# Attention output divided without transposes: denominators sent through DMA, SyncE queue in source order

## Chip, cores, metric

The kernel runs on one core of a Trainium2 chip. The metric is the device time of one execution in microseconds, median of three runs. TensorE is written PE below, VectorE DVE, ScalarE ACT, GpSimd POOL, SyncE SP.

## What is computed

Eight sequences of 512 tokens with 512 channels go through a "macaron" block: half a feed-forward layer, attention, half a feed-forward layer, each behind a layer norm and added to its input.

```python
x = x + 0.5 * ffn(layernorm(x))        # ternary weights, silu(gate) * up, rms norm
x = x + attention(layernorm(x))        # 32 heads of 16 channels, window of 128 keys back
x = x + 0.5 * ffn(layernorm(x))
# attention, for each head and block of 128 queries:
probs = softmax(where(valid, q @ k.T / 4, min))
out   = (probs @ v) @ Wo.T
```

The softmax is computed as weights exp(score - maximum). Their products with v, and their sum (the denominator), come out of the same matmul; the output is the product divided by the denominator. The change is about where that division is done.

## The kernel before

There are three stages. Stage a (first feed-forward) writes `rows_a` to HBM, stage b (attention) reads `rows_a` and writes `rows_b`, and stage c (second feed-forward) reads `rows_b`. All matmuls are fp32 or fp32 in split terms.

Stage b treats the 8 sequences (index `b`) by groups of 8 heads (index `j`, 4 to a sequence): 32 groups `i`. A group has four units `u`, one for each block of 128 queries (index `t`), so there are 128 units. The source is one loop over `u`, a software pipeline written out by hand. One pass of the loop, called a step here, emits in this order:

- `probabilities(u)`: PE forms score tiles `sp` (line 798). ACT takes three and DVE one of the four out of PSUM (lines 810 and 806), ACT takes the exponential (812), POOL zeroes what lies outside the window in two halves (817).
- `weighted(u - 1)`: PE multiplies the weights by `vones`, which holds 16 columns of v and 16 columns of ones for each head, into `av` (833). In this way 16 rows of `av` are the product and 16 rows the denominator, 32 rows for each of 4 heads. Each second unit ACT copies `av` to `ab` (842).
- `maxima(u + 6)`: PE forms the scores `sm` (750), and DVE takes their maximum in 8 instructions named `seen` (758), each followed by a short read of the accumulator.
- one long product of 8 matmul instructions (line 677), by `t`: values (`wv`) at t = 0, output (`wo`) at t = 1, queries (`wq`) at t = 2, keys (`wk`) at t = 3. The queries and keys are for group `i + 3`; they are split in two terms by ACT and DVE (690, 691), and SP issues four DMAs `qs` (708) or four DMAs `ks` (720) that interleave them over partitions.
- after each second unit `turned` (851): four PE transposes of `ab` into `abT`; `divided` (857, 861): DVE takes reciprocals of the denominators and multiplies four times; and one step later `turned_back` (873, 876): two PE transposes back, and an ACT copy into `oT`.
- `row_loaded(b + 2)` (641): an SP DMA that loads 1 MB of `rows_a` into `x_b`, at j = 0, t = 3. `x_b` has one buffer. The layer norm of it begins in the next step (j = 1, t = 0) with `st_b` on DVE (204), and goes on over j = 1 and 2.
- `output(b - 1, j)` at t = 1: `wo` reads `oT`, DVE adds the residual `xr` (890), SP stores to `rows_b` (891).

Score tiles, transposes and the `neg` transposes (777) share six PSUM buffers `ps_s`, given out in turn; `av` and the long products have one each.

PE, DVE, ACT and POOL run the loop in source order (`manual_schedule`). SP is not in that list: the framework's scheduler places SP's DMAs. On every engine instructions run strictly in the built order, so a waiting instruction holds up all behind it. DMAs take one of eight completion semaphores in turn, so each DMA also waits for the one eight before it.

Of the kernel before, what the change touches and what calls it, by code (L numbers as in the profile page):

```python
# [8 lines left out]
F32 = mybir.dt.float32  # L9
# [3 lines left out]
ALU = mybir.AluOpType  # L13
AX = mybir.AxisListType

P = 128
# [8 lines left out]
def macaron_block(  # L25
# [19 lines left out]
    nc = tc.nc  # L45
# [41 lines left out]
    rows_b = [dram.tile([P, TB, D], F32, name=f"rows_b{b}") for b in range(B)]  # L87
    wgu_kept = [dram.tile([P, 2 * DC, P], F32, name=f"wgu_kept{c}") for c in range(FC)]
    h_kept = [dram.tile([P, T], F32, name=f"h_kept{c}") for c in range(FC)]
    wp_kept = [dram.tile([P, 2, D], F32, name=f"wp_kept{u}") for u in range(FC // 2)]  # L90

    PSUM = bass.MemoryType.PSUM

    def pool(stack, name, bufs, space=bass.MemoryType.SB):

        return stack.enter_context(
            tc.tile_pool(name=name, bufs=bufs, space=space, reuse_waits="tile")
        )
# [511 lines left out]
    def attention_stage():  # L610
# [16 lines left out]
        }  # L627
        ring = pool(s, "ring_b", 3)
        probs = pool(s, "probs_b", 3)
        opool = pool(s, "o_b", 7)  # L630
        work = pool(s, "work_b", 3)

        ps_s = pool(s, "ps_s", 6, PSUM)
# [11 lines left out]
        attn_w = {}  # L645
        for name, src in (("wv", wv_t), ("wq", wq_t), ("wk", wk_t), ("wo", wo_t)):
            attn_w[name] = fixed[name].tile([P, DC, D], F32, name=f"{name}_sb")
            nc.sync.dma_start(attn_w[name], src.rearrange("(c p) e -> p c e", p=P))
        vones = [
            fixed[f"vones{i}"].tile([P, TB, N_HEADS, 2 * DK], F32, name=f"vones{i}_sb")  # L650
            for i in range(2)
# [6 lines left out]
        for h in range(2):  # L658
            nc.vector.tensor_copy(selects[h], max_rows[h].to_broadcast([P, P]))
        for tile_ in vones:  # L660
            nc.gpsimd.memset(tile_[:, :, :, DK:], 1.0)
        for tile_ in terms_of_negs:
            nc.gpsimd.memset(tile_.bitcast(F32), 0.0)

        xrs = {}
        abTs, qs, ks, ms, pTs, avs, abs_, os_, oTs = {}, {}, {}, {}, {}, {}, {}, {}, {}
        NJ = DC
        units = B * NJ * TB

# [3 lines left out]
        def sum_of_products(name, pairs, done):  # L673
            space, tag = (ps_mm, "mm") if 0 <= u < units else (ps_s, "s")
            ps = space.tile([P, T], F32, tag=tag, name=name)
            for n, (lhs, rhs) in enumerate(pairs):
                nc.tensor.matmul(ps, lhs, rhs, start=(n == 0), stop=(n == len(pairs) - 1))  # L677
            done(ps)
# [45 lines left out]
        def values(b, t):  # L724
            rows = slice(t * P, (t + 1) * P)
            pairs = [(xss[b][:, k, rows], attn_w["wv"][:, k, :]) for k in range(DC)]
            sum_of_products(
                f"wv_{b}_{t}", pairs,
                lambda ps: nc.vector.tensor_copy(
                    vones[b % 2][:, t, :, :DK], ps.rearrange("p (h d) -> p h d", d=DK)  # L730
                ),
            )

        def scores_tile(name):
            return [
# [87 lines left out]
        def weighted(u):  # L823

            i, t = u // TB, u % TB
            b, j = i // NJ, i % NJ
            if t % 2 == 0:
                avs[i] = ps_av.tile([P, 2, 2, P], F32, tag="av", name=f"av_{u}")
            for h in range(2):
                blocks = [(t - 1, 1), (t, 0)] if t else [(t, 0)]  # L830
                for n, (block, m) in enumerate(blocks):
                    for g in range(NG):
                        nc.tensor.matmul(  # L833
                            avs[i][32 * g : 32 * g + 32, h, t % 2, :],
                            vones[b % 2][:, block, NG * (2 * j + h) + g, :],
                            pTs[u - t + block][:, 2 * g + h, m * P : (m + 1) * P],
                            start=(n == 0), stop=(n == len(blocks) - 1),
                        )

            if t % 2 == 1:  # L840
                abs_[i] = work.tile([P, 2, 2, P], F32, tag="ab", name=f"ab_{u}", bufs=2)
                nc.scalar.copy(abs_[i], avs.pop(i))

        def turned(u):

            i, t = u // TB, u % TB
            pt = abTs[i] = ps_s.tile([P, 2, 2, P], F32, tag="s", name=f"abT_{u}")
            ab = abs_.pop(i)
            for m in range(2):
                for h in range(2):  # L850
                    nc.tensor.transpose(pt[:, m, h, :], ab[:, h, m, :], ident)  # L851

        def divided(u):
            i, t = u // TB, u % TB
            rows = abTs.pop(i).rearrange("p m h (g r) -> p (m h) g r", r=32)
            rden = small.tile([P, 4, NG, 1], F32, tag="rden", name=f"rden_{u}")
            nc.vector.reciprocal(rden, rows[:, :, :, DK : DK + 1])
            os_[i] = work.tile([P, 2, 2, NG, DK], F32, tag="o", name=f"o_{u}", bufs=2)
            for m in range(2):
                for h in range(2):  # L860
                    nc.vector.tensor_tensor(
                        os_[i][:, m, h], rows[:, 2 * m + h, :, :DK],
                        rden[:, 2 * m + h].to_broadcast([P, NG, DK]), ALU.mult,
                    )

        def turned_back(u):
            i, t = u // TB, u % TB
            if t == 1:
                oTs[i] = opool.tile([P, T], F32, tag="oT", name=f"oT_{i}")
            o = os_.pop(i)  # L870
            back = ps_s.tile([P, 2, P], F32, tag="s", name=f"oTp_{u}")
            for m in range(2):
                nc.tensor.transpose(
                    back[:, m, :], o[:, m].rearrange("p h g d -> p (h g d)"), ident
                )
            nc.scalar.copy(
                oTs[i][:, (t - 1) * P : (t + 1) * P], back.rearrange("p m q -> p (m q)")
            )

        def residual_loaded(b, t):  # L880
            xrs[b, t] = work.tile([P, D], F32, tag="xr", name=f"xr_{b}_{t}")
            nc.scalar.dma_start(xrs[b, t], rows_a[b][:, t, :])

        def output(b, t):
            xr = xrs.pop((b, t))
            rows = slice(t * P, (t + 1) * P)
            pairs = [(oTs[NJ * b + j][:, rows], attn_w["wo"][:, j, :]) for j in range(NJ)]

            def done(ps):
                nc.vector.tensor_tensor(xr, ps, xr, ALU.add)  # L890
                nc.sync.dma_start(rows_b[b][:, t, :], xr)

            sum_of_products(f"wo_{b}_{t}", pairs, done)
# [2 lines left out]
        row = NJ * TB  # L896
        engines = {
            mybir.EngineType.PE, mybir.EngineType.DVE, mybir.EngineType.Activation,
            mybir.EngineType.Pool,
        }  # L900
        s.enter_context(tc.manual_schedule(engines=engines))
        for u in range(-row - row // 2 - 2, units + row):
            i, t = u // TB, u % TB
            b, j = i // NJ, i % NJ
            if b == -2 and j == 2:
                with tc.high_priority():
                    if t == 0:
                        for block in range(TB):
                            norms[0][0](block)
                    for part in norms[0][1:]:  # L910
                        part(t)
            if 0 <= u < units:
                probabilities(u)
            if 0 <= u - 1 < units:
                weighted(u - 1)
            if t == 0 and 0 <= b - 1 < B:
                residual_loaded(b - 1, j)
            ended = u - 1 + AHEAD
            if 0 <= ended < units and ended % TB == TB - 1:

                maxima_split(ended // TB)
            if 0 <= u + AHEAD < units:
                maxima(u + AHEAD)
            if j in (1, 2) and 0 < b + 2 < B:
                norms[b + 2][j - 1](t)

            if 0 <= ended < units and ended % TB == TB - 1:
                maxima_turned(ended // TB)
            if b == -1 and j >= 2 and t < 2:
                values(0, 2 * (j - 2) + t)  # L930
            if t == 0 and 0 < b + 1 < B:
                values(b + 1, j)
            if t == 1 and 0 <= b - 1 < B:
                output(b - 1, j)
            if t == 2 and 0 <= i + 3 < B * NJ:
                queries(i + 3)
            if t == 3 and 0 <= i + 3 < B * NJ:
                keys(i + 3)
            turned_b, turned_t = divmod(u - 1, row)
            turned_t -= 2 * TB  # L940
            if 0 <= turned_t < TB and 0 < turned_b + 2 < B:
                norms[turned_b + 2][2](turned_t)
            if 0 <= u - 1 < units and (u - 1) % 2 == 1:
                turned(u - 1)
                divided(u - 1)
            if 0 <= u - 2 < units and (u - 2) % 2 == 1:
                turned_back(u - 2)
            if j == 0 and t == 3 and 0 < b + 2 < B:
                row_loaded(b + 2)
        s.close()  # L950
# [32 lines left out]
```

## Time and profile before

| | us |
|---|---|
| median of 3 runs (2469.08 to 2471.29) | 2469.84 |
| the profiled execution | 2469.46 |
| its span, first to last instruction | 2467.4 |
| mean granted PE clock | 0.98 of full |
| busy: PE, DVE, ACT, POOL | 2379.9, 1339.4, 982.2, 861.8 |

The span runs from the first to the last instruction; the execution is 2.06 us longer. Stage b lies between about 800 us, when stage a's last rows are ready, and 1719 us, when stage c's first rows are loaded. In the profile lines, `x8` is a count of instructions, and a name such as `abT<-ident,ab` is output from inputs.

### The profile page before, as it was taken

To read this page: it belongs to the slowest core of one execution; us is meant where nothing else is said; L and a number is where in the kernel's file an instruction comes from. 1 tells how busy PE (TensorE), PEld (TensorE's weight loads), DVE (VectorE), ACT (ScalarE), POOL (GpSimd) and SP (SyncE) were. 2 spreads that over 40 slices of the span, in tenths; PEclk is the share of its full clock that TensorE was granted. 3 is DMA by queue.
4 is the path that set the end of the run, shared out by engine and by line. 5 is a ranking of instruction groups with operands and counts; after the bars stand their busy time and mean duration, and the time that the engine had idled before them with its cause. 6 is when DMAs were issued, how large, how long until landed. Compare 5 with 4: busy or idle time off the path is not lost.

```text
span 2467.4 us, 43216 instructions
## 1 busy us (share of the span) xinstructions
PE 2379.9 (96%) x17208; PEld 1777.0 (72%) x17208; DVE 1339.4 (54%) x3929; ACT 982.2 (40%) x1476; POOL 861.8 (35%) x714
## 2 busy tenths in 40 slices
PE   5999999999999999999999999987899999999998
PEld 4778888888887466666666666654788888888887
DVE  7884443443444676766767676662444453453442
ACT  6773222222221355665556566554222222222221
POOL 0000344444445132323223232222344444444544
PEclk8999999999999999999999999988899999999999
DMA  4433010000011523323332332353100000100000
GB/s 162 157 135 135 35 35 1 35 35 1 35 52 37 143 58 84 105 74 95 83 95 74 96 91 74 78 159 135 58 35 1 35 35 1 35 35 1 35 18 17
DMA packets 63192, 160.58 MB, mean 65 GB/s; under 512 B 7440, under 2 KB 11536, under 8 KB 59920
## 3 DMA queue, kind: packets, MB, share of 16 engines
q1 hardware_dynamic: 47680, 116.68, 16.4%
q10 hardware_dynamic: 15312, 41.16, 4.5%
q8 instruction: 135, 2.21, 0.4%
q14 instruction: 65, 0.53, 0.1%
HBM read 66.32 MB, written 41.16 MB: 44 GB/s over the span
## 4 chain that ended last, share of the span: by engine, by line
PE 92%; DVE 3%; ACT 2%; issue 1%; DMA 0%; POOL 0%; ACTq 0%; POOLq 0%; DVEq 0%; SPq 0%
PE gu_c L281 19%; PE gu_a L281 17%; PE o_a L316 9%; PE o_c L316 9%; PE sp L798 5%; PE wk L677 5%; PE wv L677 5%; PE av L833 5%; PE wo L677 5%; PE wq L677 5%; PE sm L750 4%; PE abT L851 1%; PE neg L777 1%; ACT pT L812 1%; PE ptn_c L225 1%
## 5 line engine op out<-in xcount | busy, mean ns | idle before, releaser
L281 PE MATMUL gu_a<-xs_a,wgu_a 128*128 128x512 f32 x2048 | 493.3, 394 | 7.2 <-ACT sg_a L292 3.0
L281 PE MATMUL gu_c<-xs_c,wgu_c 128*128 128x512 f32 x2048 | 490.1, 392 | 0.7 <-ACT xs_c L228 0.7
L817 POOL TENSOR_SCALAR_AFFINE_SELECT pT<-pT 128x1024 f32<-128x1024 f32 x224 | 242.8, 1104 | 628.6 <-ACT pT L812 628.6
L281 PEld LDWEIGHTS gu_a<-xs_a,wgu_a 128*128 128x128 f32 x2048 | 383.6, 189 | 90.1 <-ACT sg_a L292 4.3
L281 PEld LDWEIGHTS gu_c<-xs_c,wgu_c 128*128 128x128 f32 x2048 | 383.1, 188 | 80.1 <-ACT xs_c L228 1.1
L758 DVE CUSTOM_DVE_ANT_0 seen<-sm,window 128x256 f32<-128x256 f32 (+1 forms) x1024 | 331.3, 388 | 87.4 <-PE sm L750 86.6
L316 PE MATMUL o_a<-wp_a,hs_a 128*128 128x512 f32 x1024 | 256.6, 396 | 0.0
L316 PE MATMUL o_c<-wp_c,hs_c 128*128 128x512 f32 x1024 | 251.6, 389 | 0.0
L297 DVE TENSOR_TENSOR h_c<-gu_c,sg_c 128x512 f32<-128x512 f32 x128 | 88.3, 690 | 277.9 <-PE gu_c L281 275.7
L587 POOL TENSOR_TENSOR sq_c<-h_c 128x512 f32<-128x512 f32 x120 | 124.9, 1041 | 316.5 <-DVE h_c L297 303.1
L810 ACT ACTIVATE pT<-sp 128x512 f32<-128x512 f32 (+1 forms) x384 | 181.2, 545 | 129.6 <-PE sp L798 129.6
L316 PEld LDWEIGHTS o_a<-wp_a,hs_a 128*128 128x128 f32 x1024 | 193.3, 190 | 40.0 <-DVE hs_a L306 0.2
L812 ACT ACTIVATE pT<-pT 128x2048 f32<-128x2048 f32 (+1 forms) x128 | 217.3, 1698 | 10.9 <-DVE pT L806 7.6
L316 PEld LDWEIGHTS o_c<-wp_c,hs_c 128*128 128x128 f32 x1024 | 192.2, 188 | 39.9
L297 DVE TENSOR_TENSOR h_a<-gu_a,sg_a 128x512 f32<-128x512 f32 x128 | 88.3, 689 | 230.2 <-PE gu_a L281 225.6
L588 POOL TENSOR_TENSOR ss_c<-ss_c,sq_c 128x512 f32<-128x512 f32 x120 | 192.1, 1601 | 8.9
L292 ACT ACTIVATE sg_c<-gu_c 128x512 f32<-128x512 f32 x128 | 76.6, 599 | 263.9 <-PE gu_c L281 248.6
L302 ACT CAST hs_c<-h_c 128x512 fp32r<-128x512 f32 x128 | 79.5, 621 | 250.2 <-DVE h_c L297 250.1
L587 POOL TENSOR_TENSOR sq_a<-h_a 128x512 f32<-128x512 f32 x90 | 94.1, 1045 | 229.9 <-DVE h_a L297 220.7
L306 DVE TENSOR_TENSOR hs_c<-h_c,hs_c 128x512 fp32r<-128x512 f32 x128 | 124.1, 969 | 83.1 <-ACT hs_c L302 83.1
L292 ACT ACTIVATE sg_a<-gu_a 128x512 f32<-128x512 f32 x128 | 76.4, 597 | 212.3 <-PE gu_a L281 202.8
L302 ACT CAST hs_a<-h_a 128x512 fp32r<-128x512 f32 x115 | 71.3, 620 | 202.4 <-DVE h_a L297 200.0
(137 smaller groups left out, 3128.1 us busy)
## 6 DMA issues: line engine op xcount, KB each, us to landing
ks<-k SPq DMA_DIRECT2D x128, 256.0 KB, 4.9
qs<-q SPq DMA_DIRECT2D x128, 128.0 KB, 2.4
wf_gu<-w_gate_up_dram SPq DMA_DIRECT2D x16, 512.0 KB, 3.5
wgu_kept<-wgu_a ACTq DMA_DIRECT2D x16, 512.0 KB, 2.7
rows_a<-x_a ACTq DMA_DIRECT2D x8, 1024.0 KB, 3.9
x_b<-rows_a SPq DMA_DIRECT2D x8, 1024.0 KB, 5.4
xr<-rows_a ACTq DMA_DIRECT2D x32, 256.0 KB, 5.4
rows_b<-xr SPq DMA_DIRECT2D x32, 256.0 KB, 2.1
```

Source lines behind the costliest of these rows:

```text
L281: nc.tensor.matmul(ps, wgu[c][:, i * DC + k, :], xss[b][:, part, k, :], start=(k == 0 and part == 0), stop=(k == DC - 1 and part == 1),)
L292: nc.scalar.activation(sg, gate, AF.Silu)
L297: nc.vector.tensor_tensor(h, up, sg, ALU.mult)
L302: nc.scalar.copy(hs[:, 0, :], h)
L316: nc.tensor.matmul(ops[t], hs[:, part, t * P : (t + 1) * P], wp[e // 2][:, e % 2, :], start=(e == begin and part == 0), stop=(e == end and ...
L587: nc.gpsimd.tensor_tensor(sq, h, h, ALU.mult)
L588: nc.gpsimd.tensor_tensor(sumsq, sumsq, sq, ALU.add)
L677: nc.tensor.matmul(ps, lhs, rhs, start=(n == 0), stop=(n == len(pairs) - 1))
L758: nc.vector.tensor_tensor_reduce(out=seen[:, : n * P], in0=tiles[g][:, h, : n * P], in1=window[:, (2 - n) * P :], scale=-1.0, scalar=3.4e3 ...
L810: nc.scalar.activation(under, tiles[g][:, :, : n * P], AF.Relu, scale=-1.0)
L812: nc.scalar.activation(seen, seen, AF.Exp, scale=-1.0)
L817: nc.gpsimd.affine_select(out=half, in_=half, compare_op=ALU.is_ge, fill=0.0, base=0, pattern=[[0, 2 * NG], [sign, P]], channel_multiplier ...
```

## The change

- `vones` holds v and ones in alternate columns: v first for half of the heads (h = 0), ones first for the others. Its memset covers the whole tile, and the copy of `wv` into it becomes two strided copies of half the size. Product rows of h = 0 then lie on even partitions of `av`, those of h = 1 on odd ones.
- `turned`, `divided` on DVE, and `turned_back` are gone. ACT copies `av` into `sums`, one tile for a whole group.
- Once for each group, SP sends one denominator row per head to HBM (`dens`, two DMAs) and both halves of the product rows into one tile `oT` (two DMAs of 128 KB); loads the denominators back as 128 x 32 (`den`); DVE takes 128 x 32 reciprocals; SP writes them to HBM (`inverses`) and reads each row back 16 times over into `rep` (eight DMAs of 32 KB); POOL multiplies `oT` by `rep`. These stand one or two steps apart, over the two groups that follow.
- Output products come two groups later, and the loop is eight steps longer. `wo` is loaded in two halves with rows in the new order. `oT` has 9 buffers (7 before), `xr` 2 (3 before).
- SP joins the engines whose order is that of the source.

```diff
-        opool = pool(s, "o_b", 7)
+        opool = pool(s, "o_b", 9)
...
-            nc.gpsimd.memset(tile_[:, :, :, DK:], 1.0)
+            nc.gpsimd.memset(tile_, 1.0)
...
+            def kept(ps):
+                heads = vones[b % 2][:, t].rearrange("p (j h g) d -> p h j g d", h=2, g=NG)
+                made = ps.rearrange("p (j h g d) -> p h j g d", h=2, g=NG, d=DK)
+                for h in range(2):
+                    nc.vector.tensor_copy(heads[:, h, :, :, h::2], made[:, h])
...
             if t % 2 == 1:
-                abs_[i] = work.tile([P, 2, 2, P], F32, tag="ab", name=f"ab_{u}", bufs=2)
-                nc.scalar.copy(abs_[i], avs.pop(i))
...
+                if t == 1:
+                    sums[i] = work.tile([P, 2, T], F32, tag="sums", name=f"sums_{i}", bufs=2)
+                nc.scalar.copy(
+                    sums[i][:, :, (t - 1) * P : (t + 1) * P],
+                    avs.pop(i).rearrange("p h m q -> p h (m q)"),
                 )
+        def rows_of(t, h):
+            return t.rearrange("(r two) t -> r two t", two=2)[:, h]
+        def denominators(i):
+            taken = sums.pop(i)
+            for h in range(2):
+                nc.sync.dma_start(
+                    dens[i % 2][h],
+                    taken[:, h].rearrange("(g r) t -> g r t", r=32)[:, 1 - h],
+                )
+            oTs[i] = opool.tile([P, T], F32, tag="oT", name=f"oT_{i}")
+            for h in range(2):
+                nc.sync.dma_start(rows_of(oTs[i], h), rows_of(taken[:, h], h))
+        def denominators_back(i):
+            den = dens_sb[i] = work.tile([P, T // DK], F32, tag="den", name=f"den_{i}", bufs=1)
+            nc.sync.dma_start(den, dens[i % 2].rearrange("h g (s e) -> (h g s) e", s=DK))
+        def inverted(i):
+            inv = work.tile([P, T // DK], F32, tag="inv", name=f"inv_{i}", bufs=1)
+            nc.vector.reciprocal(inv, dens_sb.pop(i))
+            nc.sync.dma_start(inverses[i % 2].rearrange("h g (s e) -> (h g s) e", s=DK), inv)
+        def spread(i, h):
+            if h == 0:
+                reps[i] = work.tile([P, T], F32, tag="rep", name=f"rep_{i}", bufs=1)
+            rows = rows_of(reps[i], h)
+            for g in range(NG):
+                nc.sync.dma_start(
+                    rows[DK * g : DK * (g + 1)],
+                    inverses[i % 2][h, g].unsqueeze(0).to_broadcast([DK, T]),
+                )
+        def divided(i):
+            nc.gpsimd.tensor_tensor(oTs[i], oTs[i], reps.pop(i), ALU.mult)
...
-            mybir.EngineType.Pool,
+            mybir.EngineType.Pool, mybir.EngineType.SP,
         }
-        for u in range(-row - row // 2 - 2, units + row):
+        for u in range(-row - row // 2 - 2, units + row + 2 * TB):
...
+            out_b, out_t = divmod(i - NJ - 2, NJ)
+            if 0 <= i - 1 < B * NJ:
+                if t == 0:
+                    denominators(i - 1)
+                if t == 1:
+                    denominators_back(i - 1)
+                if t == 2:
+                    inverted(i - 1)
+                if t == 3:
+                    spread(i - 1, 0)
+            if 0 <= i - 2 < B * NJ:
+                if t == 0:
+                    spread(i - 2, 1)
+                if t == 2:
+                    divided(i - 2)
...
-            if t == 1 and 0 <= b - 1 < B:
-                output(b - 1, j)
+            if t == 1 and 0 <= out_b < B:
+                output(out_b, out_t)
...
-            if 0 <= u - 1 < units and (u - 1) % 2 == 1:
-                turned(u - 1)
-                divided(u - 1)
-            if 0 <= u - 2 < units and (u - 2) % 2 == 1:
-                turned_back(u - 2)
```

More of the change, by code (lines that the diff above doesn't have):

```diff
@@ L89, in macaron_block @@
     h_kept = [dram.tile([P, T], F32, name=f"h_kept{c}") for c in range(FC)]
+    dens = [dram.tile([2, NG, T], F32, name=f"dens{n}") for n in range(2)]
+    inverses = [dram.tile([2, NG, T], F32, name=f"inverses{n}") for n in range(2)]
     wp_kept = [dram.tile([P, 2, D], F32, name=f"wp_kept{u}") for u in range(FC // 2)]
@@ L647, in attention_stage @@
             attn_w[name] = fixed[name].tile([P, DC, D], F32, name=f"{name}_sb")
-            nc.sync.dma_start(attn_w[name], src.rearrange("(c p) e -> p c e", p=P))
+            if name != "wo":
+                nc.sync.dma_start(attn_w[name], src.rearrange("(c p) e -> p c e", p=P))
+                continue
+            by_half = src.rearrange("(c h r) e -> h r c e", h=2, r=P // 2)
+            for h in range(2):
+                nc.sync.dma_start(
+                    attn_w[name].rearrange("(r two) c e -> r two c e", two=2)[:, h], by_half[h]
+                )
         vones = [
@@ L665, in attention_stage @@
         xrs = {}
-        abTs, qs, ks, ms, pTs, avs, abs_, os_, oTs = {}, {}, {}, {}, {}, {}, {}, {}, {}
+        qs, ks, ms, pTs, avs, sums, dens_sb, reps, oTs = {}, {}, {}, {}, {}, {}, {}, {}, {}
         NJ = DC
@@ L726, in values @@
             pairs = [(xss[b][:, k, rows], attn_w["wv"][:, k, :]) for k in range(DC)]
[L727 to L732, printed above, removed]
+            def kept(ps):
[3 more added lines that the diff above has]
+                    nc.vector.tensor_copy(heads[:, h, :, :, h::2], made[:, h])
+            sum_of_products(f"wv_{b}_{t}", pairs, kept)
         def scores_tile(name):
@@ L840, in weighted @@
             if t % 2 == 1:
-                abs_[i] = work.tile([P, 2, 2, P], F32, tag="ab", name=f"ab_{u}", bufs=2)
-                nc.scalar.copy(abs_[i], avs.pop(i))
[L844 to L874, printed above, removed]
-                )
-            nc.scalar.copy(
-                oTs[i][:, (t - 1) * P : (t + 1) * P], back.rearrange("p m q -> p (m q)")
-            )
+                if t == 1:
+                    sums[i] = work.tile([P, 2, T], F32, tag="sums", name=f"sums_{i}", bufs=2)
@@ new lines, in weighted @@
+                nc.scalar.copy(
+                    sums[i][:, :, (t - 1) * P : (t + 1) * P],
+                    avs.pop(i).rearrange("p h m q -> p h (m q)"),
+                )
+        def rows_of(t, h):
[8 more added lines that the diff above has]
+            oTs[i] = opool.tile([P, T], F32, tag="oT", name=f"oT_{i}")
+            for h in range(2):
+                nc.sync.dma_start(rows_of(oTs[i], h), rows_of(taken[:, h], h))
@@ new lines, in denominators_back @@
+        def denominators_back(i):
[10 more added lines that the diff above has]
+            for g in range(NG):
+                nc.sync.dma_start(
+                    rows[DK * g : DK * (g + 1)],
+                    inverses[i % 2][h, g].unsqueeze(0).to_broadcast([DK, T]),
+                )
@@ L880, in residual_loaded @@
+        def divided(i):
+            nc.gpsimd.tensor_tensor(oTs[i], oTs[i], reps.pop(i), ALU.mult)
         def residual_loaded(b, t):
-            xrs[b, t] = work.tile([P, D], F32, tag="xr", name=f"xr_{b}_{t}")
+            xrs[b, t] = work.tile([P, D], F32, tag="xr", name=f"xr_{b}_{t}", bufs=2)
             nc.scalar.dma_start(xrs[b, t], rows_a[b][:, t, :])
@@ L915, in attention_stage @@
                 weighted(u - 1)
-            if t == 0 and 0 <= b - 1 < B:
-                residual_loaded(b - 1, j)
+            out_b, out_t = divmod(i - NJ - 2, NJ)
+            if t == 0 and 0 <= out_b < B:
+                residual_loaded(out_b, out_t)
+            if 0 <= i - 1 < B * NJ:
[12 more added lines that the diff above has]
+                    divided(i - 2)
             ended = u - 1 + AHEAD
```

## Prediction, made before the changed kernel ran

> **What bounds the kernel now.** The chain that ended last is read first, for the engine; then the windows, for where that engine is full; then the chain in order of time.
>
> ```profile
> PE 92%; DVE 3%; ACT 2%; issue 1%; DMA 0%; POOL 0%; ACTq 0%; POOLq 0%; DVEq 0%; SPq 0%
> ```
> ```profile
> 1060.00:1160.00 100.00, 100.00 (x1176) 61.23 (x1166) 71.06 (x334) 59.20 (x88) 28.80 (x27) 1.00 0.36 94
> 1600.00:1706.00 106.00, 88.46 (x1198) 58.98 (x1194) 53.76 (x258) 62.17 (x92) 31.08 (x29) 0.84 0.40 125
> ```
> ```profile
> 1153.33 0.44 PE abT L851 x4
> 1153.77 0.91 PE sp L798 x21
> 1154.68 0.57 PE av L833 x16
> 1155.25 1.04 PE sm L750 x16
> 1156.29 3.63 PE wo L677 x8
> 1159.92 0.22 PE oTp L873 x2
> 1160.14 0.91 PE sp L798 x23
> ```
>
> The columns of the windows are length, then busy time of PE, PE's weight loads, DVE, ACT and POOL, then clock and DMA share. In the steady part of attention PE has no idle time and a full clock, and nobody else is over 71%: what leaves PE leaves the time. From 1600 us on the values, queries and keys run out, PE idles and its clock is 0.84: here latency sets the time. Four turns cost 0.44 us of chain, two turns back 0.22.
>
> Three more views show what else the change touches: SP's queue around a load of `x_b` with its landing time, the end of stage b, and the entry to it.
>
> ```profile
> 1145.74 0.33 SPq L641 DMA_DIRECT2D x_b<-rows_a  x1
> 1147.39 4.04 SPq L720 DMA_DIRECT2D ks<-k  x4
> ```
> ```profile
> DMA to landing us min/median/max: 4.9/5.4/6.5
> ```
> ```profile
> 1704.91 0.91 PE av L833 x24
> 1706.48 0.66 PE abT L851 x4
> 1707.14 3.44 PE wo L677 x8
> 1710.80 6.88 PE wo L677 x16
> 1717.70 0.70 DVE xr L890
> 1719.38 8.59 DMA x_c<-rows_b
> ```
> ```profile
> 788.85 1.82 POOL vones_sb L661
> ```
>
> `x_b` is issued ahead of `ks` as soon as its one buffer is free (its wait is for the last `xn_b`), two groups before DVE needs it; no `st_b` waits for it in the steady part.
>
> **The change, part by part**, against the profiled execution (2469.46; the median is 0.4 above it).
>
> Transposes. A group loses 2 x 0.44 + 2 x 0.22 = 1.32 us of PE. Steady groups, 28 of 32: -36.9. The last four come under the tail. Cover check: a step without them is 6.15 (t = 1) to 6.57 us. From the start of `sp` to where `av` needs POOL's first half is 1.07 to the first ACT copy, 1.58, 1.91, 1.1 and some 0.2, 5.9 us, against a step plus 0.9: it still fits. ACT loses 0.37 x 64, DVE 2.2 us a group.
>
> Output two groups later. Groups 4 and 5 have no `wo`. Where the step before lacked it (groups 1 to 3), t = 1 took 4.83 to 5.04 us (882.13 to 886.96; 907.49 to 912.53), held by ACT. So each saves 6.15 - 4.6, about 1.5: -3. Bounds 0 and -7.3 (two products at 3.63). The two products come back behind the last unit, under a wait.
>
> SP in source order. The built order puts `x_b` behind the four `ks`, one step before `st_b`, which now waits for the DMA. Times from the start of `sp` at t = 0: `ks` is issued 1.4 after the end of `wk` (1118.80 to 1120.19) and takes 3.12; `x_b` goes out at 4.5 and lands 5.4 later, 9.9. DVE then has `st_b` with its mean (0.9 with gaps), the two copies into `vones` (0.75, from one at 0.69), and the fourth score copy (0.69): done at 12.4. Before it would be 6.24 + 1.04 + 0.69 = 8.0. PE's `sm` of that step needs that buffer (the waits name it: `sm` for DVE `pT`, 26 times up to 0.4 us), and everything of PE is queued behind. So PE stands 4.4 us, for six loads (rows 2 to 7; that of row 1 lies in the ramp). After the idle 2.43 us at 1608.7 four turns took 0.66 instead of 0.44 and `wo` 4.17 instead of 3.63, so I add 0.4 for part of that 0.8: 6 x 4.8 = +29. Bounds: a landing of 4.9 gives 3.9 without re-warming, +23. If `x_b` moves only when the `ks` traffic is over (DMA busy until 1182.1, 7.1 us after the first `ks` issue, so 8.5 here) and then at the 406 GB/s of its best microsecond, 2.6 for 1 MB, it lands at 11.1: 5.6 and 0.8 re-warming, +38. And 0, if `sm` is held by something else.
>
> [...]
>
> Denominators by DMA. A group gets 14 issues more: two `dens`, two `oT`, one `den`, one `inverses`, eight `rep`. At 0.33 (a store of `rows_b`) and 0.6 (a `qs`, for the `oT`) that is 12 x 0.33 + 2 x 0.6 = 5.2 us of SP, which issues for 5.9 of 26.8 now. The waits in SP's queue: `dens` for ACT's copy (4.43 + 0.57 = 5.0 after the step's start), `rep` for `ks` landings until 9.3, `den` out at 9.5, then `rows_b` for `xr` at 13.3, `inverses` for DVE at 14.5, `qs` at 20.2 as before. The shortest landing in the trace is 2.0, that of 128 KB `qs` 2.4; nothing as small as 16 KB is shown, so a small one is between 1 and 5 (the `ks`); I take 2.4, as the nearest. `den` lands at 12.0. DVE comes to the reciprocal at 14.2 and would idle until 15.0 for `seen` anyway: 3.0 us cover, cost nothing. If the cover is gone, DVE waits with `seen` and the next score copy behind it, and PE after them, 28 times. POOL's multiply (between 1.04, one input, and 1.60, two inputs, in stage a) stands between two selections with 4.4 us idle: nothing. The first four `rep` of a group go out at 24 of 25.4, ahead of `ks`: no delay there.
>
> Tail. From 1632.97 (unit 116) to the end of `av` at 1705.8 are 72.9 us. PE waited for ACT's `ab` here, as the exponential of the next unit stands before it on ACT. Without turns: three steps with `wo` about 6.9, four with `seen` (8 x 0.47 + 0.69 = 4.4 DVE) and their turns of buffers 5.3, five bound by ACT (1.58 + 1.91 + half of 0.57 + gaps) 3.9: 61.4, so -11.5; group 28, whose t = 0 has no values, -2.5. Bounds of the sum -6 and -18. Then the new chain behind the last `av`: copy 0.75; SP issues `dens`, `oT`, four `rep` (3.2), `den` 2.2, reciprocal 0.4, `inverses` 2.2, eight `rep` 2.6 and landing 2.2, multiply 1.5: 15.1; three products at 4 and the addition: 28 until `x_c` is issued, against 13.5 now: +14.5 (+10 with cheap landings, +20 with `wp_c` loads of 512 KB between). `x_c` then meets an empty queue: 5.4 for 8.59, -3 (0 to -4). Tail: -2.5.
>
> Memset. POOL's first memset lies on the chain; twice the elements at the same rate: +1.8 (0 if a contiguous one is faster). The second has 7.4 us idle behind it. Halves of `wo`, buffer counts, two copies for one: an issue of 0.37 and some 0.1 us DVE, hidden.
>
> Sum: -36.9 - 3 + 29 - 2.5 + 1.8 = -11.6, so 2457.9; I give 2458.
>
> **The rivals.**
>
> Full gain: `st_b` stalls but PE does not, because its cover is larger than read. For it: PE meets DVE's copy only at the fourth tile of `sm`. Against: all PE work is queued behind. Time: 2469.5 - 36.9 - 3 - 2.5 + 1.8 = 2429.
>
> Cancelled: `x_b` lands behind all of the `ks` and PE re-warms in full, the upper bound of 38 instead of 29: 2467; with a tail at its bound of +20 about 2473. For it: the DMA engines are full while `ks` move. Against: the median landing, which was also taken beside `ks`.
>
> Slower, by one mechanism: the reciprocal's wait on DVE at t = 2. If `den` lands later than 15.0, three small transfers deep in SP's queue, each group stands; at 16.5 it is 28 x 1.5 = +42: 2500. It decides against the gain from 15.4 on (28 x 0.4). For it: 9.5 rests on `ks` landing, whose largest is 7.4 instead of 4.9. Against: 3.0 us of cover.
>
> That the transposes stay is excluded: the built order lacks all 384.
>
> **How the numbers follow.** Forecast, gain partly eaten (2440 to 2464): 0.50. Full gain: 0.15. Cancelled (2464 to 2485): 0.17. Reciprocal late: 0.18. This kernel's measurement tells about 0.2%, 5 us, from no change. Faster by that: all of full gain, 0.45 of the forecast: 0.60. Same: 0.05 of the forecast and 0.09 of cancelled: 0.14. Slower: 0.26. The range takes most of full gain, and cancelled, and the near part of the late reciprocal: 2430 to 2488.
>
> **What would show it.** Right: no `abT` or `oTp`; steady groups of 25.4 us; six DVE waits of 3 to 5 us "`st_b` <- DMA `x_b`" with PE idle at `sm`; no DVE wait at the reciprocal outside these groups; 15 us between the last `av` and `wo`. Wrong: no such waits of `st_b`, or 28 waits for `den`, or POOL late at `pT`.

## The result and the profile after

| | us |
|---|---|
| before | 2469.89 (2469.08 to 2471.29) |
| after, median of 4 runs | 2497.39 (2490.65 to 2501.07) |
| ratio, 95% interval | 1.0108 [1.0086, 1.013] |
| forecast, range | 2458.0, 2430 to 2488 |

The change makes the kernel 27.5 us slower; the forecast had the wrong sign, and the time lies above the range. The profiled execution of after took 2501.07 us (span 2499.3), so the account below, made on the two spans, has to come to +31.9. The shares of the chain that ended last come first.

```profile
PE 84%; DMA 5%; DVE 4%; ACT 3%; SPq 2%; issue 1%; POOL 1%; ACTq 0%; POOLq 0%; DVEq 0%
```

PE had 92% of this chain and has 84%; DMA had none and has 5%, some 125 us. The windows (length; busy time of PE, weight loads, DVE, ACT, POOL; clock; DMA share; GB/s) show the same steady stretch as before, and then the inside of the group that begins at 1103.10:

```profile
1060.00:1160.00 100.00, 93.29 (x1105) 54.00 (x1103) 63.38 (x296) 53.89 (x78) 34.28 (x31) 0.97 0.39 102
1105.00:1109.00 4.00, 3.89 (x49) 2.08 (x48) 1.02 (x6) 1.62 (x5) 2.14 (x2) 1.00 0.97 263
1109.00:1113.00 4.00, 0.73 (x13) 0.53 (x13) 0.00 (x0) 0.43 (x1) 0.00 (x0) 0.86 0.88 291
1113.00:1116.00 3.00, 0.37 (x1) 0.37 (x2) 1.94 (x5) 0.00 (x0) 0.00 (x0) 0.50 0.17 56
```

PE is no longer full. From 1109.8 to 1114.0 all engines stand still, while the DMA engines are 88% busy (97% in the window before), and by the time work comes back the granted clock is 0.50. SP's queue at this point, and DVE's waits over the whole run (total us, times, longest):

```profile
1101.88 3.17 SPq L729 DMA_DIRECT2D ks<-k  x4
1105.09 1.79 SPq L643 DMA_DIRECT2D x_b<-rows_a  x1
1106.97 1.28 SPq L868 DMA_DIRECT2D dens<-sums  x2
1108.30 1.35 SPq L874 DMA_DIRECT2D oT<-sums  x2
1109.70 4.80 SPq L890 DMA_DIRECT2D rep<-inverses  x4
1114.61 0.52 SPq L878 DMA_DIRECT2D den<-dens  x1
```
```profile
DVE st_b L206 <- DMA x_b<-rows_a: 50.9, 7, 8.8
DVE inv L882 <- DMA den<-dens: 7.7, 6, 3.0
```

`x_b` goes out behind `ks`, as foreseen, but `st_b` could start only when `x_b` had landed at 1114.00, 8.9 us after the issue. PE's next instruction after the pause is `wo`, and what it waited for is DVE's copy of the product before it, `wv`, into `vones`:

```profile
1115.63 5.22 PE L686 MATMUL wo<-wo_sb,oT 128*128 128x512 f32 x8 [5.90 <-DVE vones_sb L742]
```

The end of stage b, from the chain in order of time (start, length, what):

```profile
1717.22 5.21 DMA wp_c<-wp_kept
...
1724.35 1.96 DMA den<-dens
...
1727.62 7.52 DMA wp_c<-wp_kept
...
1738.68 7.50 DMA xr<-rows_a
...
1751.48 8.23 DMA x_c<-rows_b
```

Last, the entry to stage b: POOL's second memset, and the small DVE instruction `half_a` beside it.

```profile
800.72 3.51 POOL L670 MEMSET vones_sb<- 128x4096 f32 x1
800.80 3.45 DVE L342 TENSOR_SCALAR half_a<-rms_a 128x4 f32<-128x4 f32 x1 [1.13 <-POOL rms_a L191]
```

The account, with "group" the time from one group's first exponential to the next one's:

| part | forecast | profile |
|---|---|---|
| up to the first exponential (852.94, after 860.04) | +1.8 | +7.1 |
| groups 0 to 27 without `x_b`'s six | -39.9 | -28.3 |
| the six groups that wait for `x_b` | +29 | +40.2 |
| units 112 to 127 (the tail's steps) | -14 | -9.1 |
| last exponential to `x_c`'s issue (16.7, after 38.8) | +14.5 | +22.1 |
| `x_c`'s landing and all behind it | -3 | -0.2 |
| sum | -11.6 | +31.8 |

The forecast's -39.9 covers all 28 groups. The six measured ones compare with the same six of before (25.35 the first, the others about 26.76). The saving of 1.3 belongs to them too, so a load costs 40.2 / 6 + 1.3 = 8.0 on average, together 48.

### The profile page after: what moved, and what is told of

Same layout as the page of the kernel before. It is cut to its first block, busy times and chain, and to the rows that moved or that the text cites. A ratio compares the mean times of both kernels' runs of the same rounds, so it can differ in the third digit from the quotient of the medians.

```text
span 2499.3 us, 42903 instructions
## 1 busy us (share of the span) xinstructions
PE 2357.4 (94%) x16824; PEld 1736.0 (69%) x16824; DVE 1301.1 (52%) x3673; ACT 962.1 (38%) x1412; POOL 904.7 (36%) x746
## 4 chain that ended last, share of the span: by engine, by line
PE 84%; DMA 5%; DVE 4%; ACT 3%; SPq 2%; issue 1%; POOL 1%; ACTq 0%; POOLq 0%; DVEq 0%
PE gu_c L283 19%; PE gu_a L283 17%; PE o_c L318 9%; PE o_a L318 8%; PE wq L686 5%; PE wk L686 5%; PE sp L810 4%; PE wo L686 4%; PE av L845 4%; PE wv L686 4%; PE sm L762 3%; DMA x_b<-rows_a 2%; ACT pT L822 1%; PE neg L789 1%; SPq L729 1%
## 5 line engine op out<-in xcount | busy, mean ns | idle before, releaser
L829 POOL TENSOR_SCALAR_AFFINE_SELECT pT<-pT 128x1024 f32<-128x1024 f32 x224 | 242.4, 1103 | 595.8 <-ACT pT L824 595.8
L318 PEld LDWEIGHTS o_c<-wp_c,hs_c 128*128 128x128 f32 x1024 | 192.2, 188 | 39.9
L686 PE MATMUL wo<-wo_sb,oT 128*128 128x512 f32 x256 | 133.5, 672 | 35.1 <-DVE vones_sb L742 24.7
```

What stands on the lines that cost most here:

```text
L318: nc.tensor.matmul(ops[t], hs[:, part, t * P : (t + 1) * P], wp[e // 2][:, e % 2, :], start=(e == begin and part == 0), stop=(e == end and ...
L829: nc.gpsimd.affine_select(out=half, in_=half, compare_op=ALU.is_ge, fill=0.0, base=0, pattern=[[0, 2 * NG], [sign, P]], channel_multiplier ...
```

## The experiments

**Which half of the change costs.** `e1_old_sp_order` is the kernel before with only SP put in source order; `e2_sp_by_scheduler` is the changed kernel with only that undone.

```diff
-            mybir.EngineType.Pool,
+            mybir.EngineType.Pool, mybir.EngineType.SP,
```

> The kernel before with only SP added to the engines that keep source order; the transposes stay and there are no denominator DMAs. Theory (the place of the x_b load in SP's queue is what costs): x_b goes out behind the four ks, DVE waits for it in st_b six times for 4 to 8 us with PE behind it, so 2470 + 6 x (4 to 7) = 2494 to 2512. Rival (x_b is only slow because of the new traffic of the denominators): small waits of st_b, 2470 to 2480.

> The changed kernel with SP taken out of the engines that keep source order, so that the scheduler places SP's DMAs as before; all else of the change stays. Theory (x_b's place): the load goes out two groups early again, the six waits of st_b (48 us) go, 2497 - 48 = 2449, with some us more if the eight rep of a group, now all ahead of qs, hold SP. Rival (the denominators' chain through DMA is what costs, wherever it stands): 2485 or more.

Measured: e1 2516.61, 1.0193 [1.0176, 1.021], 46 us over its own runs of before; e2 2455.61, 0.9948 [0.9929, 0.9967]. Source order alone costs 46 us without any of the new transfers. In e2 the waits for `x_b` are gone; two long steps remain in it (13.1 and 14.2 us at t = 2 of groups 7 and 11, where DVE waits for `den`), to which e12 below comes back. DVE's waits in e1:

```profile
DVE st_b L204 <- DMA x_b<-rows_a: 44.4, 6, 8.1
```

**Is it `x_b`'s place?** The load is written earlier, so that it stands earlier in SP's order: in `e3_xb_early` at the end of the step j = 2, t = 3 of the row before, right ahead of `dens` and `den`; in `e5_xb_behind_den` two steps later, behind `den`; `e6_old_division_xb_early` gives e1 the place of e3.

```diff
-            xt = xpool.tile([P, TB, D], F32, tag="x", name=f"x_b{b}")
-            nc.sync.dma_start(xt, rows_a[b])
+            if b not in xts:
+                row_fetched(b)
...
+            if j == 2 and t == 3 and 0 < b + 3 < B:     # e5: j == 3 and t == 1
+                row_fetched(b + 3)
```

> The changed kernel with SP in source order, but the DMA of x_b is written in the source at j = 2, t = 3 of the sequence before (right behind the last read of its buffer), instead of j = 0, t = 3; the rest stays. Theory (x_b's place): 2497 - 48 = 2449, x_b groups of 25.4 us like the others. Rival (source order hurts SP in general, by qs, ks or the denominators): 2475 or more, and clearly slower than with SP placed by the scheduler.

> The changed kernel, SyncE in source order, with x_b's transfer written one step past the reciprocal's read: at the end of step t = 1 of the fourth group of the row before, behind dens, den and the row's store in SyncE's queue. Theory (1 MB costs whatever small transfer stands right behind it, and here that is inv and rep, which have two steps of cover): the six x_b groups fall from 31-34.6 to about 25.4 us (-48 on the changed kernel) and the t = 2 steps of groups 7, 11, 15, 19 stay at 6.05, so 2445 to 2453. Rival (any place in one queue's order costs about the same, since rep and GpSimd's product come late and the selects queue behind the product): the stalls move to t = 2 or t = 3 of the following group and the time is 2465 to 2480, like the placing right ahead of dens (2471).

> The kernel before (division by transposes) with SyncE in source order and x_b's transfer three groups earlier (end of t = 3 of the third group of the row before). Here no denominators pass through SyncE's queue. Theory (all that source order costs is x_b's place): back to 2468 to 2472, no st_b wait on x_b, x_b groups at 26.8. Rival (source order itself costs, through qs, ks or rows_b waiting behind one another): 2485 to 2510, between this and the 2516.6 of the old division with SyncE in source order.

Measured: e3 2471.22, 1.0009 [0.9987, 1.003]; e5 2448.72, 0.9914 [0.9897, 0.9932]; e6 2471.81, 1.0008 [0.9998, 1.0018]. e6 shows that `x_b`'s place is all that source order cost the old kernel. e5 shows that it is worth 48.7 us in the changed one, near six times 8.0 (between the two profiles, the six groups give 44.3 of it). In e3 only half came back: the t = 2 steps of groups 3, 7, 11, 15 and 19 took 9.1 to 14.8 us in place of 6.05, 28 us in sum (some 25 without what group 3 has in after too, 9.3). The chain of e3 in group 11:

```profile
1149.49 10.00 DMA x_b<-rows_a
1159.49 0.02 issue
1159.50 0.49 SPq L896
...
1160.09 3.52 DMA den<-dens
1163.61 0.02 issue
1163.63 0.35 DVE inv L888
1163.99 0.95 DVE neg_terms L786
...
1166.62 1.09 PE neg L795 x4
```

The last of four `rep` issues (L896) waits until `x_b` has landed: behind `x_b` come two `dens`, two `oT` and four `rep`, and the fourth `rep` is the eighth, which uses `x_b`'s semaphore again. `den` stands behind it, DVE waits at the reciprocal for `den`, and PE behind DVE. DVE's waits in these five groups are 12 us and PE's pauses behind them 17; the rest is matmuls at a lower clock (in group 11 `wq` took 5.95 for 3.44, at 0.50 to 0.61). That is the rival "reciprocal late" of the prediction, in five groups.

**Cover for the reciprocal.** `e8_steps_later` is e5 with the denominators' steps moved; `e10_xb_early_steps` makes the same edit to e3, `e12_free_steps` to e2.

```diff
-                if t == 2:
-                    inverted(i - 1)
                 if t == 3:
-                    spread(i - 1, 0)
+                    inverted(i - 1)
             if 0 <= i - 2 < B * NJ:
-                if t == 0:
-                    spread(i - 2, 1)
-                if t == 2:
+                if t < 2:
+                    spread(i - 2, t)
+                if t == 3:
                     divided(i - 2)
```

> As the kernel with x_b behind den, and the denominators' chain spread over more steps: reciprocal at t = 3 in place of 2, the two halves of rep at t = 0 and 1 of the next group, the product at t = 3. Theory (groups 3, 4 and 5 lose 3.3, 3.7 and about 1.5 us because den is late for a reciprocal one unit behind it): these go to 6.0-6.9, 8 us less in the groups, less about 3 to 6 us for one step more in the tail's chain: 2 to 5 us below the kernel with x_b behind den. Rival (those steps are held by something else, such as PE's own work or the late clock): the same time as it, or up to 6 us more by the tail alone.

> The kernel with x_b's transfer right ahead of dens and den (2471.2), and the denominators' steps one unit later (reciprocal at t = 3). Theory (its five long t = 2 steps of 9.1 to 14.8 us are VectorE standing at the reciprocal for den behind 1 MB, and a unit more of cover takes most of it): the t = 2 steps of groups 3, 7, 11, 15, 19 within 2 us of 5.84, t = 3 of those longer by 0 to 3, 2431 to 2442. Rival (den is not what those steps wait for; the 1 MB slows PE's operands, qs or ks): the long steps stay and the time is 2450 to 2460, only the 18 us lower that the later steps gave elsewhere.

> The changed kernel with SyncE ordered by the scheduler (2455.6) and the denominators' steps one unit later. Theory (what source order costs is x_b's place alone, and what the scheduler's order still lost was den late for the reciprocal, t = 2 steps of 13.1 and 14.2 in groups 7 and 11): 2428 to 2436, level with the kernel in source order with x_b behind den. Rival (the scheduler's order sets other transfers in front of inv or rep, and GpSimd's product comes late instead): 2440 to 2455.

Measured: e8 2431.02, 0.9845 [0.983, 0.986]; e10 2437.43, 0.9868 [0.9844, 0.9892]; e12 2444.95, 0.9887 [0.9865, 0.9909]. In e10 the five long steps are 5.84 to 6.86. DVE's waits at the reciprocal, in e3 and then in e10:

```profile
DVE inv L888 <- DMA den<-dens: 16.3, 10, 3.7
```
```profile
DVE inv L888 <- DMA den<-dens: 2.5, 1, 2.5
```

So one unit more of cover is enough here even for a `den` behind 1 MB. In e12 the two long steps of e2 are 5.84 too, as its theory says. But it is 14 us above e8: some 10 in group 30 (28.5 for 18.7), where ScalarE stood 7.9 us for a DMA, and 6 in groups 0 to 5, most of which had stretches at half clock. Its rival had the time and not this cause. The 18 us of e8 over e5 were more than expected: each group from 6 on is 0.2 us shorter (some 4 us in all; the reciprocal has moved from t = 2 to t = 3 of DVE), group 30 6.7, and groups 1 to 5 some 9 us, but these last for another reason. The granted clock over 880 to 1010 us was 1.00 in most windows of e8 and 0.86 to 0.93 in e5; in `e11_all`, which has the same steps, it was 0.86 to 0.93 again and these groups were as long as in e5. These are averages: the clock records of these runs hold 0.50 and 1.00 alone, and each low window has stretches of 3.4 or 6.8 us at 0.50 in it. e4 and e14, which do not move the steps, had no such stretch over groups 3 and 4, and these lasted 24.3 and 24.1 to 24.2 us there, as in e8 (24.3 and 24.0). So they are as short without the later steps, where the clock holds, and the gain that e8's theory gave to `den` there is not shown. What sets off a stretch at half clock in one run and not in the other is open.

**Why `x_b` takes 8.9 us to land.** `e9_xb_on_act` issues it at the same place of the source from ScalarE; there it left 4.5 us sooner, as it did not stand behind the issues of `ks`. `e14_xb_late_on_act` issues it from ScalarE right behind the exponential that opens the group.

```diff
-            nc.sync.dma_start(xt, rows_a[b])
+            (nc.scalar if b > 1 else nc.sync).dma_start(xt, rows_a[b])
```

> The changed kernel with x_b's transfer of rows 2 to 7 at the same place in the source but issued by ScalarE, so on another queue than the four ks transfers that it stands behind. Theory (the prediction sized the x_b stall with 5.4 us from issue to landing, and it is 8.3 to 9.7 because the 1 MB waits in one queue behind 1 MB of ks): landing back to 5 to 6 us, each of the six x_b stalls 3 us shorter, 2476 to 2482. Rival (what delays it is the bandwidth that both share, or the late place alone): landing still 8 to 9 us, time 2494 to 2500.

> The changed kernel with x_b of rows 2 to 7 issued by ScalarE right behind the t = 0 exponential of the group that needs it, about 2 us after that exponential's start: the moment at which SyncE issued it behind ks in the changed kernel. Theory (one queue serves in order, and 8.9 us is 1 MB behind what is left of ks's 1 MB): it lands in 5.0 to 6.0 us, the six stalls fall from 8 to 4.5-5.2 us each, 2476 to 2482. Rival (the bandwidth is shared whatever the queue): it lands in 8 to 9.5 us and the time stays at 2494 to 2500.

Measured: e9 2448.95, 0.9912 [0.9897, 0.9927]; e14 2495.88, 1.0091 [1.0058, 1.0124]. In e9 the load and the first `st_b` behind it:

```profile
1084.34 0.33 ACTq L643 DMA_DIRECT2D x_b<-rows_a  x1
1090.06 0.69 DVE L206 BATCH_NORM_STATS2 st_b<-x_b 128x6 f32<-128x512 f32 x1 [0.23 <-DMA x_b<-rows_a]
```

and in e14, the same group in the chain:

```profile
1094.92 10.32 DMA x_b<-rows_a
```

e9's time lies below both forecasts, since the load left sooner and DVE hardly waited for it, and it can't tell the theories apart, as start and queue changed together. e14 decides: on a queue of its own, issued 2 us sooner within the group than in the changed kernel, the load took 9.9 to 11.6 us in five of six groups and ended at about the same point of the group. To move it to another queue gained nothing (2495.88 for 2497.39). `x_b` and `ks`, 1 MB each, share DMA engines that the windows show full (97 and 88% busy in the changed kernel, 91% in e14 from 1095 to 1103); started before `ks`, `x_b` was through in 5.7.

The packets in the traces (8 KB each for `x_b`, 4 KB for `ks`) show how they share. In the changed kernel, on one queue, 235 to 241 of the 256 `ks` packets have started when the first of `x_b` does, 2.3 to 3.2 us after the issue, and `x_b` then needs 5.1 to 6.0 us. In the kernel before, its first packet started 1.0 us after the issue, and in four loads that had the engines almost to themselves it needed 3.6 to 3.7. In e14, on two queues, the two are mixed: in five of six groups half of `ks` starts ahead of `x_b` and most of the rest among its packets.

**The memset.** `e4_ones_only` sets only the columns of ones; `e11_all` adds this to e8.

```diff
-            nc.gpsimd.memset(tile_, 1.0)
+            by_head = tile_.rearrange("p t (j h g) d -> p t j h (g d)", h=2, g=NG)
+            for h in range(2):
+                nc.gpsimd.memset(by_head[:, :, :, h, 1 - h :: 2], 1.0)
```

> The changed kernel with the memset of vones over the columns of ones alone (two strided memsets of a quarter of the tile each, so half the elements), as many elements as before the change. Theory (both memsets lie on the way: the first ahead of the squares on POOL, the second beside DVE's half_a, which took 3.46 us under it instead of 1.75): 1.7 + 1.7 us less between stage a's last product and ptn_b, 2494. Rival (only the first is on the way): 1.7 less. A difference this small is read from the profile, not from the time.

> x_b behind den, the denominators' steps one unit later, and only the columns of ones set by the memset. Theory (half_a stands 1.6 us less behind GpSimd's memset, the two memsets on the path shorter): 3 to 4 us below 2431.0, so 2426 to 2429. Rival (the ramp's few us are lost in the spread of the first stage's clock): within 1.5 us of 2431.

Measured: e4 2498.69, 1.0118 [1.0093, 1.0143]; e11 2436.64, 0.9865 [0.9851, 0.988]. No gain in either time: a few us at the entry are below what the clock of the first stage (from 60 to 120 us 0.95 in e8, 0.91 in e11, 0.86 in after) and of groups 1 to 5 moves from run to run. The profile of e4 does show the step:

```profile
796.95 1.92 POOL L672 MEMSET vones_sb<- 128x1024 f32 x2
797.03 1.86 DVE L342 TENSOR_SCALAR half_a<-rms_a 128x4 f32<-128x4 f32 x1 [1.13 <-POOL rms_a L191]
```

`half_a`, 4 elements to a partition, ends with the memset: 1.75 us beside one of 1.80 before, 3.45 beside 3.51 after, 1.86 beside 1.92 here. It runs eight times in a kernel; with no memset beside it the median is 0.17.

**The chain at the end.** `e7_four_residuals` gives `xr` four buffers, with room from `sums` (one in place of two). `e13_weights_on_act` issues the last stage's weight loads from ScalarE; `e15_steps_weights` does this to e8.

```diff
-                    nc.sync.dma_start(wgu[c].bitcast(F32), wgu_kept[c])
+                    nc.scalar.dma_start(wgu[c].bitcast(F32), wgu_kept[c])
...
-                        nc.sync.dma_start(wp[c // 2].bitcast(F32), wp_kept[c // 2])
+                        nc.scalar.dma_start(wp[c // 2].bitcast(F32), wp_kept[c // 2])
```

> The changed kernel with four xr buffers in place of two (room for them from sums, one buffer in place of two). Theory (in the end chain the last outputs wait for their residual rows, each loaded only when the store two before it has landed, 7.5 us): the xr waits of 4.9 and 3.4 us at the end go, x_c issues 6 to 7 us sooner, 2489 to 2492 against 2497.4. Rival (the chain is set by the eight rep transfers on SyncE and their landing): within 1.5 us of the changed kernel. A third possibility is a cost from the single sums buffer: the t = 1 copy on ScalarE would wait for a DMA, steps at t = 2 longer, over 2500.

> The changed kernel with the last stage's weight loads (wgu_c, wp_c, 512 KB each) issued by ScalarE in place of SyncE. Theory (in the end chain SyncE's rep, den and row stores wait behind those loads: 5.2 and 7.5 us of wp_c stand in the chain): from the last exponential to x_c's issue 30 to 34 us in place of 38.8, 2488 to 2493. Rival (the chain is the denominators' own round trips, their issues of 0.59 us and the four cold output products): 37 to 40 us, time within 2 us of 2497; a third way is that ScalarE's exponentials of the last groups stand behind its own blocked loads, over 2500.

> x_b behind den and the denominators' steps one unit later (2431.0), and the last stage's weight loads issued by ScalarE. Theory as for the same edit to the changed kernel: the chain from the last exponential to x_c falls from 37.5 to 30-34 us, 2424 to 2428. Rival: within 2 us of 2431, or above it where ScalarE stands behind its loads.

Measured: e7 2495.65, 1.0112 [1.0092, 1.0133]; e13 2509.07, 1.0148 [1.0131, 1.0166]; e15 2455.69, 0.9932 [0.9914, 0.9951]. From the last exponential to `x_c`: 39.5 in e7, 42.9 in e13, 42.7 in e15, against 38.8 in after and 37.5 in e8. In e7 the time stayed, as the rival said; in e13 and e15 it was the third way. In e7 the wait for `xr` was in the shadow of PE, which after 10.8 us of idle time had a granted clock of 0.77 on average (1736 to 1746) and needed 14 us for what was left of the last four products:

```profile
1735.43 13.99 PE L686 MATMUL wo<-wo_sb,oT 128*128 128x512 f32 x26 [10.76 <-POOL oT L896]
```

In e13 no weight load stands in SP's queue, yet the chain has waits of 7.31 for `oT`, 4.51 for `den` and 6.33 for `rep`: the small transfers landed as late beside large ones of another queue (some 1 MB of weights moved on ScalarE's queue in each 4 us from 1724 to 1732). In both e13 and e15 ScalarE's copies and exponentials stood behind its own blocked loads as well (group 29 took 28.0 and 27.8, 19.5 and 21.0 without the edit).

## Why the prediction was wrong

- **Transposes** (-36.9): right. Plain steady groups are 25.44 in place of 26.74, 1.30 each, 1.32 forecast.
- **SP in source order** (+29, bounds 23 and 38): this is the step that failed first. That `x_b` would go out behind `ks`, and DVE and PE stand for it six times, was right, and so was the issue 4.5 us after `sp` (1100.42 to 1105.09, 4.7). "Lands 5.4 later" was wrong: it took the landing from loads of before, which were issued ahead of `ks`, and used it for a load behind 1 MB of `ks`. There it was 8.3 to 9.7. Wrong too was the place where PE stands. `sm` of that step ran to its end, 9.3 us after `sp` in the group shown and not 8.0; in four of six groups PE then stood at `wo`, until DVE had copied `wv` out of the one buffer of the long products, which comes one DVE copy sooner than the `pT` that the forecast named. In the other two, which have no `wo`, it stood at the next `sp`, for `pT`. So a landing 3.5 us later made PE's pause only 1.7 longer, 6.1 us on average for 4.4. With 1.5 from the next line, these are the 3.2 us missing for each load, 19 in all. The upper bound was too low as well: it let `x_b` land 11.1 us after `sp`, and it landed after 13.6. It took the rate of one good microsecond (406 GB/s, where the view's best is 418), and the windows show 263 to 291.
- **Re-warming** (0.4 a stall): too small; what a load costs beyond PE's pause is 8.0 - 6.1 = 1.9. The product behind the 5.9 us of idle time took 5.22 for 3.63, and the step with it (t = 1) was 7.2 to 8.4 for 6.15 in the four groups that have a `wo`. The granted clock was 0.50 from 1111.9 to 1118.7 us; it fell 2.2 us after PE's last matmul. The first 3.1 us of that product lie in this stretch; half of them, 1.5, is an estimate of the loss, beside the 1.6 measured.
- **Output two groups later** (-3): in this profile groups 4 and 5 gained nothing. t = 1 did get shorter (3.93 and 4.47), and t = 2 took it back (9.71 and 7.87). In group 4 the clock was at 0.50 from 975.4 to 982.2, over that step. In e4 and e14 it stayed at 1.00 through this group, and the group lasted 24.1 and 24.2 us, 1.2 to 1.3 less than a plain 25.44. So the gain is there at a full clock, near the 1.5 forecast, and lost at half clock.
- **Denominators** (0, and a rival at 0.18): right for plain groups; the rival's mechanism is real as soon as 1 MB is issued ahead of `den` (e3), through the semaphore eight transfers on. The prediction counted that wait for `ks` and not for `x_b`.
- **Tail** (-2.5): steps -9.1 for -14. Behind the last `av`, copy to multiply took 21.2 for 15.1 (1717.37 to 1738.57): a `rep` is 0.59 us of SP, not 0.33, and issues waited for 512 KB loads (`wp_c`, 5.21 and 7.52 in the chain); the three products fit, 12.9 for 13, by luck, as the chain there runs over loads of `xr` that the sum did not have. `x_c` landed in 8.23 as before, not 5.4. The forecast's worst case for this part, +20 with `wp_c` between, is near what happened (+22.1). With the steps, 15 us missing.
- **Memset** (+1.8): 1.71 for the first. The second, "7.4 us idle behind it", cost 1.70 more through `half_a` on DVE, which the forecast did not count. Another 3.6 us at the entry came in the first 120 us of stage a at a lower clock (0.86 for 0.95 from 60 to 120 us); nothing of the change is there.
- **The rivals**: "cancelled" had the cause, `x_b` behind all of `ks` with full re-warming and the tail at its bound, and priced it 2467 to 2473. Priced with the measured 8.0 for each load it comes to 2483; the rest lies in the entry, the tail and groups 4 and 5.

What is left of the change is a gain: e5 over e6, both with `x_b` out of the way, is -23 us, and with the steps one unit later the kernel is at 2431.0, 1.55% faster than before, the best version run here (2436.6 in e11 with the same steps, and half clock in groups 1 to 5). How much of the end chain's 37 us can be had back stays open, as no edit to it helped.

## What to carry over

When an engine's queue is put in source order, list its largest transfer first and ask three things: what is in flight when it starts, who needs it next, and which later transfer reuses its semaphore (in e3 the fourth `rep`). A landing time read from a profile held only for the traffic it was read in (here a median of 5.4 before, 8.3 to 9.7 behind `ks`); behind 1 MB, count what is still in flight, at the rate of a full window (here 263 to 291 GB/s), and not the median of the old loads. Ask of the stalled engine which instruction will stand, and for which buffer: that sets how much of the delay it pays (here 1.7 of 3.5 us). A round trip of small transfers paid here for what stood ahead of it (DVE waited 16.3 us at the reciprocal in e3, 2.5 in e10) and needed a unit more of cover than its own sum.

## What the runs showed that was not expected

- A DVE instruction of 4 elements to a partition lasted as long as a POOL memset that began 0.08 us before it, in three kernels (1.75 beside 1.80 in before, 3.45 beside 3.51 in after, in e4 1.86 beside two of together 1.92). `half_a` alone takes 0.17 (the median); what held it no run here shows.
- A broadcast `rep` of 32 KB cost 0.59 us of issue on SP (the median in after), almost twice the 0.33 of a 256 KB `rows_b`.
- 1 MB of `x_b` landed in 5.7 us when it started ahead of 1 MB of `ks` (e9), and in 7.4 to 11.6 (after, e1, e14), with one 6.9, when it started behind all or half of it, whichever queue issued it.
